# Sums of the first layer's softmax: TensorE products replaced by VectorE transposes and reductions for up to five of eight groups

## The chip, the core and the metric

One core of a Trainium2 chip runs the whole program. The engines have queues of their own: TensorE (PE, with weight loads as PEld), VectorE (DVE), ScalarE (ACT), GpSimd (POOL) and SyncE (SP), which issues most DMA transfers. They work side by side and wait for one another on semaphores. The metric is the device time of one execution in microseconds, the median of several runs. A profile is one execution recorded by the hardware profiler; its span is the time from the first to the last recorded instruction.

## The reference, cut to what matters

Two attention layers with a group normalisation ahead of each, on 8 batches of 32 x 32 positions (1024 tokens) with 512 channels, all in float32. The first layer has 16 heads of width 32, the second 4 heads of width 128 with position logits added to its scores.

```python
def _L0_conv_ref(x, w_qkv, w_proj, b_proj):      # first layer
    qkv = xt @ w_qkv                             # [B, 1024, 3 * 512], 16 heads of 32
    attn = jnp.einsum('bhid,bhjd->bhij', q * SCALE, k)
    attn = jax.nn.softmax(attn, axis=-1)
    out = jnp.einsum('bhij,bhjd->bhid', attn, v)
    out = out @ w_proj + b_proj
...
x = x + _L0_conv_ref(_gn(x), ...)
x = x + _L1_conv_ref(_gn(x), ...)                # second layer, with position logits
```

The softmax is computed without subtracting a maximum: the exponentials are summed over the keys, the unnormalised output is divided by that sum, and a bound on the sums is checked at the end of the program. The change is about the sums of the first layer.

## The kernel before, in words

**The order of the whole.** The program goes through the batches. Attention of the first layer for batch b is woven with other work: the second layer of batch b-1, and the first layer's projections for batch b+1. The weave is written out in the program: `side_by_side` takes steps of `attention_0` and, after each, as many pieces from the chain of other work as the costs that the pieces yield say. A piece of the other work is mostly one product of a projection: `seven` (L497) makes a projection from seven smaller products, into the PSUM tiles x (two), y (three) and z (two) (the names a, b, p with _q, _k, _v in the profile are the temporary tiles of that scheme). The products of one projection are issued by L421, sixteen records of the profile for one product; sums of products are made by VectorE (L511 a, L519 b), copies by ScalarE (L506, L525 p) and the last addition by GpSimd (L680). TensorE executes its instructions in the order in which the program lists them.

**Attention of the first layer** (`attention_0`, L796). A group is (m, h): four heads (m, in the order 0, 2, 1, 3) and one half of the queries (h, 512 of them); there are 8 groups per batch, numbered 0 to 7 here, and 64 in the program. Each group goes over 8 key blocks j of 128 keys. One step does:

- L809: scores of 128 keys by 512 queries for four heads, in `ps`, the one wide tile of PSUM (four banks)
- L824: their exponential, by ScalarE, from `ps` to a slot of `e_room`
- one step later, L835: four products with v, added up in `acc`
- L847: VectorE adds the exponentials to the group's first ones. After eight blocks that slot, `esum`, holds for each of four heads (`r`) the sums over the blocks, and 128 partitions are still to be added up.

**`e_room`** has three slots of 128 x 4 x 512. A group's first block takes a slot that stays its `esum`; the other two slots take turns. At the next group's first block its slot becomes the new sum slot and the old sum slot joins the turn; in it the next group's third block (j = 2) is written. So that exponential waits until the old `esum` has been read.

**The end of a group** (`finish`, L853, and `normalise`, L749). When the next group begins, TensorE multiplies `esum` by a matrix of ones, four products of 32 columns for the four heads (L857), which gives the sums over partitions, repeated in 32 partitions for each head, in a PSUM tile of the tag "acc". ScalarE copies them (L755), VectorE transposes them in blocks of 32 x 32 (L757), takes the reciprocal of one column in 32 (L772), records its bound (L775), and spreads it again by a transposing copy (`spread`, L787). GpSimd multiplies the output, which lies in `q`, with it (L761).

**The second layer** sums in another way. `added_up` (L763) transposes the 128 x 512 sum in blocks of 32 x 32 (L766) and reduces each run of 32 to one number (L767), which leaves 128 x 16 in `few`. `fold_up` (L1003) adds up the partitions that belong together by one product with the constant `fold` (L1008) for many groups at once, and inverts the result (L772). Then `quotient` (L1016) spreads each group's reciprocal (L787) and multiplies, on GpSimd or VectorE (L1024). For most batches the fold is in `closing` and the eight quotients in `quotients` (L1151); both run beside the first layer's projections for the coming batch, two quotients at a time, issued after the projection's VectorE instruction that `half_done` or `closed` names.

**The tag "rec"** is a ring of two tiles of 128 x 512. All of these take their tiles from it in turn: `su` and `tu` of `normalise`, the transposed tiles of `added_up`, the spare tiles of the folds, and the spread quotients of both layers. A tile that is asked for waits until the last reader of the tile before it in the same place is done; for a spread quotient that reader is the multiplication on GpSimd.

**Weights** come by DMA, issued by SP, into a ring of 16 tiles of the tag "w" (class `Stream`, L215).

## Time and profile before

| | |
|---|---|
| median of 3 runs | 3642.09 us (3640.19 to 3643.6) |
| profiled execution, its own time | 3640.86 us |
| span of the profile | 3639.1 us, clock 1.00 throughout |
| records of PE | 33882 |
| L857 sums | 512 records in 64 groups, 71.0 us busy |
| L755 copy of the sums (ACT) | 64, mean 585 ns |
| L757 transpose (DVE) | 64, mean 704 ns |
| L772 reciprocal, 128 x 16 (DVE) | 64, mean 257 ns |
| L787 spread (DVE), both layers | 128, mean 686 and 706 ns |
| L761 multiplication (POOL) | 64, mean 1672 ns |
| L1024 multiplication (POOL) | 48, mean 2052 ns |
| L766 and L767, transpose and reduction of the second layer (DVE) | 64 each, mean 712 and 685 ns |
| SP | issues DMA only |

How to read it: a group of instructions is one line of the kernel on one engine with one shape, as `out<-in` with partitions x elements, then the number of its records; then its busy time in us and the mean of one in ns; then the time that the engine stood idle just before such instructions, and who ended most of that. The ends of matmuls are modelled, so neighbours overlap on paper: a product of sixteen records lasts 1.90 but the next begins 1.72 or 1.83 us after it. For costs on TensorE the distance from start to start counts. Where the timeline joins neighbouring records, it gives the first one's start, the time to the end of the last and their number.

### The profile page before, as it was taken

What the parts mean: (1) busy time and instruction counts of PE and PEld (TensorE: products, weight loads), DVE (VectorE), ACT (ScalarE), POOL (GpSimd) and SP (SyncE); (2) the same over time, 40 slices, a digit from 0 to 9 for tenths busy, and PEclk for the clock granted to TensorE, in tenths of its full rate; (3) what the DMA queues carried; (4) which work ended last, traced back from release to release, by engine and by line L of the source; (5) the groups of instructions that cost most, each with busy time, mean ns of one, the idle gap of its engine ahead of it and who ended that gap; (6) DMA issues with size and microseconds to landing.
All of it is one profiled execution on the core that took longest, in us unless ns stands there. A gap on an engine that the chain in (4) does not pass through costs nothing.

```text
span 3639.1 us, 80878 instructions
## 1 busy us (share of the span) xinstructions
PE 3617.0 (99%) x33882; PEld 1232.4 (34%) x33882; DVE 2511.6 (69%) x2710; ACT 2000.6 (55%) x2285; POOL 1385.6 (38%) x880
## 2 busy tenths in 40 slices
PE   9999999999999999999999999999999999999998
PEld 4222243222433234332343323433234332323343
DVE  6788656796567955679556795667856668567546
ACT  3555666446664466544665446654566545656254
POOL 1343155231552316523174231742318312166255
PEclk9999999999999999999999999999999999999999
DMA  6233164242643426344363443625336133325376
GB/s 192 72 111 105 42 173 137 68 141 66 185 127 89 131 62 194 112 114 113 74 195 94 136 97 96 186 75 142 84 100 198 59 100 79 96 98 157 96 203 149
DMA packets 577316, 431.96 MB, mean 119 GB/s; under 512 B 274320, under 2 KB 467632, under 8 KB 575920
## 3 DMA queue, kind: packets, MB, share of 16 engines
q1 hardware_dynamic: 567952, 411.05, 41.1%
q0 software_dynamic: 2608, 13.70, 1.0%
q8 instruction: 269, 4.41, 0.5%
q10 hardware_dynamic: 6384, 1.97, 0.2%
q14 instruction: 103, 0.84, 0.1%
HBM read 334.30 MB, written 92.27 MB: 117 GB/s over the span
## 4 chain that ended last, share of the span: by engine, by line
PE 96%; DVE 2%; issue 1%; ACT 1%; POOL 0%; DMA 0%; SPq 0%; ACTq 0%; DVEq 0%; POOLq 0%
PE ps L809 15%; PE acc L835 14%; PE ps L1053 12%; PE acc L1067 12%; PE y_v L421 5%; PE y_q L421 4%; PE y_k L421 4%; PE x_v L421 3%; PE z_v L421 3%; PE z_q L421 3%; PE x_k L421 3%; PE x_q L421 3%; PE z_k L421 3%; PE y_wp L421 2%; PE y_wo L421 2%; PE sums L857 2%
## 5 line engine op out<-in xcount | busy, mean ns | idle before, releaser
L824 ACT ACTIVATE e_room<-ps 128x2048 f32<-128x2048 f32 x512 | 962.0, 1879 | 746.4 <-PE ps L809 724.9
L847 DVE TENSOR_TENSOR e_room<-e_room 128x2048 f32<-128x2048 f32 x448 | 1100.3, 2456 | 369.4 <-ACT e_room L824 367.6
L978 POOL TENSOR_TENSOR pos<-pos,columns 128x512 f32<-128x512 f32 x448 | 637.5, 1442 | 184.7 <-DMA pos<-pr 182.8
L809 PE MATMUL ps<-q,k 32*64 32x512 f32 x8192 | 592.5, 613 | 1.6 <-ACT e_room L824 1.6
L835 PE MATMUL acc<-e_room,v 128*32 128x512 f32 x4096 | 546.8, 604 | 0.0
L1053 PE MATMUL ps<-q,k 128*128 128x512 f32 x1024 | 526.4, 597 | 0.5 <-ACT ps L987 0.5
L1067 PE MATMUL acc<-e,v 128*128 128x512 f32 x1024 | 523.0, 593 | 0.0
L1056 ACT ACTIVATE e<-ps 128x512 f32<-128x512 f32 x512 | 305.7, 597 | 315.9 <-PE ps L1053 307.0
L1083 DVE TENSOR_TENSOR es<-es,e 128x512 f32<-128x512 f32 x384 | 278.7, 726 | 289.1 <-ACT e L1056 286.5
L761 POOL TENSOR_TENSOR q<-q,su 128x512 f32<-128x512 f32 x64 | 107.0, 1672 | 505.2 <-DVE su L787 478.2
L1067 PEld LDWEIGHTS acc<-e,v 128*128 128x128 f32 x1024 | 193.3, 190 | 247.6 <-issue 133.5
L1053 PEld LDWEIGHTS ps<-q,k 128*128 128x128 f32 x1024 | 190.8, 190 | 254.3 <-issue 229.7
L987 ACT COPY ps<-pos 128x512 f32<-128x512 f32 x448 | 264.9, 592 | 0.4
L809 PEld LDWEIGHTS ps<-q,k 32*64 32x64 f32 x8192 | 122.9, 129 | 396.9 <-issue 212.7
L835 PEld LDWEIGHTS acc<-e_room,v 128*32 128x32 f32 x4096 | 81.4, 108 | 412.1 <-issue 364.1
L680 POOL TENSOR_TENSOR k<-b_k,p_k 128x512 f32<-128x512 f32 x32 | 49.7, 1553 | 417.6 <-ACT p_k L525 406.8
L680 POOL TENSOR_TENSOR v<-b_v,p_v 128x512 f32<-128x512 f32 x32 | 51.5, 1609 | 342.9 <-ACT p_v L525 315.4
L1024 POOL TENSOR_TENSOR q<-q,su 128x512 f32<-128x512 f32 x48 | 97.5, 2052 | 191.8 <-DVE su L787 191.8
L680 POOL TENSOR_TENSOR q<-b_q,p_q 128x512 f32<-128x512 f32 x32 | 56.6, 1769 | 174.5 <-ACT p_q L525 160.0
L907 ACT COPY pos<-pp 32x512 f32<-32x512 f32 x128 | 104.6, 817 | 29.2 <-PE pp L898 28.0
L1081 DVE TENSOR_TENSOR es<-e,e 128x512 f32<-128x512 f32 x64 | 59.8, 934 | 67.1 <-ACT e L1056 67.1
L757 DVE STREAM_TRANSPOSE tu<-su 128x512 f32<-128x512 f32 x64 | 45.1, 704 | 77.5 <-ACT su L755 77.5
(241 smaller groups left out, 4551.1 us busy)
## 6 DMA issues: line engine op xcount, KB each, us to landing
pos<-pr SPq DMA_DIRECT2D x448, 256.0 KB, 3.5
w_qkv<-ws_qkv SPq DMA_DIRECT2D x168, 128.0 KB, 2.7
x1T<-d SPq DMA_DIRECT2D x32, 512.0 KB, 5.2
d<-x1T SPq DMA_DIRECT2D x32, 512.0 KB, 3.6
pc<-pos SPq DMA_DIRECT2D x32, 512.0 KB, 6.5
pr<-pos SPq DMA_DIRECT2D x32, 512.0 KB, 7.7
columns<-pc SPq DMA_DIRECT2D x64, 256.0 KB, 4.3
x2T<-d SPq DMA_DIRECT2D x32, 512.0 KB, 6.0
```

Of the source, the lines that this page charges most:

```text
L421: ins = nc.tensor.matmul(out[columns, :], weights[:, columns], moving, start=start, stop=stop, skip_group_check=open_sum,)
L680: nc.gpsimd.tensor_tensor(self.dst[1][1], s(b), s(p7), op=ALU.add)
L809: nc.tensor.matmul(ps[some, r, :], k[m][rows, j * P + 64 * i : j * P + 64 * i + 64], q[m][rows, h * NB : (h + 1) * NB], start=True, stop=True,
L824: exps[0] = nc.scalar.activation(e, ps, AF.Exp, scale=D0 ** -0.5)
L835: nc.tensor.matmul(acc[r * D0 : (r + 1) * D0, :], v[:, j, c0 : c0 + D0], e[:, r, :], start=(j == blocks[0]), stop=(j == blocks[-1]),)
L847: summed[0] = nc.vector.tensor_add(state["esum"], state["esum"], e)
L978: nc.gpsimd.tensor_tensor(self.rows[i], self.rows[i], self.columns[i // NT], op=ALU.add)
L987: self.copied = nc.scalar.copy(ps, rows)
L1053: scored[0] = nc.tensor.matmul(ps, k[h][:, keys], q[:, h, queries], start=False, stop=True, skip_group_check=True)
L1056: exps[0] = nc.scalar.activation(e, ps, AF.Exp, scale=1.0 / math.sqrt(D1))
L1067: nc.tensor.matmul(acc, v[:, j, h * D1 : (h + 1) * D1], e, start=(j == 0), stop=(j == NT - 1),)
L1083: added[0] = nc.vector.tensor_add(state["esum"], state["esum"], e)
```

## The change: what it does, and the diff

For the groups in `APART` the sums are not made by `finish`. In batch 0 there are none; in batch 1 they are the parts (2, 3) and (5, 6); in batches 2 to 6 (2, 3, 4) and (5, 6); in batch 7 (3, 4). That is 4 + 25 + 2 = 31 of 64 groups. A new class `Apart` holds a part:

- `take`: while the next group's first steps run, VectorE transposes each of the four rows of `esum` (128 x 512) into a tile of the ring "rec" and reduces it to 128 x 16 in the new buffer `few_0`. Rows 1 and 2 go in the first step, rows 3 and 4 in the second, issued after the VectorE instruction that `reader[0]` names.
- `fold_up`: once per part, four products with a 32-column matrix of `fold`, one for each row r, on 48 columns (a part of three groups) or 32 (of two); then one reciprocal with its bound for the whole part.
- `quotient`: for each group of the part a spread on VectorE and a multiplication on GpSimd.

The part (2, 3, 4) of batches up to 6 is put aside (`aside`): it is folded in the second layer's `closing`, directly after that layer's own fold, and its quotients are issued among the second layer's, one after each pair. The other parts are folded and multiplied in the steps after their last group. To make room for `few_0` the weights' ring has 15 tiles in place of 16. The bound checks are counted anew.

```diff
@@ -22,6 +22,8 @@
 SUM_BOUND = 1e20
 
 BLOCKS = 8
+
+APART = [(2, 3, 4), (5, 6)]
 
 
 @with_exitstack
@@ -132,7 +134,14 @@
     for t in mvs:
         nc.gpsimd.memset(t, 0.0)
 
+
+    def apart_of(b):
+        if b == 1:
+            return [(2, 3)] + APART[1:]
+        return [] if b == 0 else [(3, 4)] if b == B - 1 else APART
+
     n_checks = B * CC * NH + 2 * 4 + B - 2
+    n_checks -= sum(len(some) - 1 for b in range(B) for some in apart_of(b))
     checks = consts.tile([P, n_checks], F32, tag="checks", name="checks")
     check_at = [0]
 
@@ -243,11 +252,11 @@
                     m.kept = None
             elif rows:
                 for c in range(HC):
-                    t = mem.tile([P, HN], F32, tag="w", name=f"w_{m.name}_{n}_{i}_{c}", bufs=16)
+                    t = mem.tile([P, HN], F32, tag="w", name=f"w_{m.name}_{n}_{i}_{c}", bufs=15)
                     nc.sync.dma_start(t, src[:, c, :])
                     got.append(t)
             else:
-                t = mem.tile([P, HC, P], F32, tag="w", name=f"w_{m.name}_{n}_{i}", bufs=16)
+                t = mem.tile([P, HC, P], F32, tag="w", name=f"w_{m.name}_{n}_{i}", bufs=15)
                 nc.sync.dma_start(t, src[:, :, u * P : (u + 1) * P])
                 got = [t[:, c, :] for c in range(HC)]
             self.tiles[n, i] = got
@@ -793,10 +802,78 @@
     e_room = mem.tile([P, 3, HB, NB], F32, tag="e0", name="e_room", bufs=1)
     turn, sum_at = [0, 1], [2]
 
+    few_0 = mem.tile([P, HB, 3, NB // 32], F32, tag="few0", name="few_0", bufs=1)
+
+    class Apart:
+
+
+        def __init__(self, b, some):
+            self.b, self.some = b, some
+            self.groups = []
+            self.width = len(some) * (NB // 32)
+
+        def place(self, r):
+            return few_0[:, r, : len(self.some), :]
+
+        def take(self, m, h, esum, dst):
+            at = len(self.groups)
+            self.groups.append((m, h, dst))
+            for r0 in range(0, HB, 2):
+                turned = []
+                for r in (r0, r0 + 1):
+                    t = mem.tile([P, NB], F32, tag="rec", name=f"tu_0_{self.b}_{m}_{h}_{r}", bufs=2)
+                    with tc.issue_after(reader[0].ins) if r0 else nullcontext():
+                        nc.vector.transpose(t, esum[:, r, :])
+                    turned.append(t)
+                for r, t in zip((r0, r0 + 1), turned):
+                    nc.vector.tensor_reduce(
+                        few_0[:, r, at, :],
+                        t.rearrange("p (t c) -> p t c", c=32),
+                        axis=AX.X,
+                        op=ALU.add,
+                    )
+                yield
+
+        def fold_up(self):
+            name = f"0_{self.b}_{self.some[0]}"
+            su = bank(f"sums_{name}")[:, : self.width]
+            for r in range(HB):
+                ins = nc.tensor.matmul(
+                    su[r * D0 : (r + 1) * D0, :],
+                    fold[:, r, :],
+                    self.place(r).rearrange("p g t -> p (g t)"),
+                    start=True,
+                    stop=True,
+                )
+                tc.keep_in_program_order(ins)
+            spare = mem.tile([P, NB], F32, tag="rec", name=f"sp_{name}", bufs=2)
+            invert(self.place(0).rearrange("p g t -> p (g t)"), su, spare[:, : self.width])
+
+        def quotient(self, i, behind=None):
+            m, h, dst = self.groups[i]
+            su = mem.tile([P, NB], F32, tag="rec", name=f"su_0_{self.b}_{m}_{h}", bufs=2)
+            with tc.issue_after(behind.ins) if behind is not None else nullcontext():
+                spread(su, few_0[:, 0, i, :])
+            nc.gpsimd.tensor_tensor(dst, dst, su, op=ALU.mult)
+
     def attention_0(q, k, v, b, blocks=range(NT)):
 
         steps = [(m, h, j) for m in (0, 2, 1, 3) for h in range(NH) for j in blocks]
         state = {}
+        aparts = {i: part for some in apart_of(b) for part in [Apart(b, some)] for i in some}
+
+        def sums_apart(i, m, h, esum):
+            part = aparts[i]
+            together = i == 4 and b < B - 1
+            if together:
+                aside.append(part)
+            yield from part.take(m, h, esum, q[m][:, h * NB : (h + 1) * NB])
+            if together or i != part.some[-1]:
+                return
+            part.fold_up()
+            for i in range(len(part.some)):
+                yield
+                part.quotient(i)
 
         def front(m, h, j):
             name = f"0_{b}_{m}_{h}_{j}"
@@ -864,14 +941,23 @@
             normalise(q[m][:, h * NB : (h + 1) * NB], su, name)
 
         pending = None
+        ended, ending = 0, []
         for at in steps:
             if "ended" in state:
-                finish(*state.pop("ended"))
+                if ended in aparts:
+                    ending.append(sums_apart(ended, *state.pop("ended")))
+                else:
+                    finish(*state.pop("ended"))
+                ended += 1
+            for part in ending:
+                next(part, None)
             e = front(*at)
             if pending is not None:
                 back(*pending)
             pending = (*at, e)
             yield 2
+        for part in ending:
+            run(part)
         back(*pending)
         yield 1
         finish(*state.pop("ended"))
@@ -1141,9 +1227,13 @@
         for _ in range(3):
             next(last, None)
 
+        aside_0 = aside.pop() if aside else None
+
         def closing():
             if together:
                 fold_up(H1 * NH - 1, f"1_{b}")
+                if aside_0 is not None:
+                    aside_0.fold_up()
             else:
                 run(last)
             yield 0
@@ -1153,6 +1243,8 @@
                 late = half_done if i // 2 % 2 == 0 else closed
                 run(quotient(i, late[0], nc.gpsimd))
                 if i % 2:
+                    if aside_0 is not None and i // 2 < len(aside_0.some):
+                        aside_0.quotient(i // 2, begun[0])
                     yield 0
 
         ends.append(closing())
@@ -1584,7 +1676,7 @@
     plan += in_parts(WO, LAST_ALONE)
 
     states = [{} for _ in range(B)]
-    ends, left = [], []
+    ends, left, aside = [], [], []
     load_first(states[0])
     WV0.add_up([nc.gpsimd] * 2 + [nc.vector] * 2, nc.gpsimd, keep=True)
     fill_fold()
@@ -1690,6 +1782,7 @@
         else:
             run(chain(*rest))
     after_last(B - 1, states[B - 1])
+    assert check_at[0] == n_checks, (check_at[0], n_checks)
 
 
     close_wide()
```

## The prediction, made before the result was known

> **What bounds the kernel now.** I read the page's first part, then the chain of waits, then the stage windows, then the groups of instructions by line and shape, then the timeline of one group change.

> ```profile
> PE 3617.0 (99%) x33882; PEld 1232.4 (34%) x33882; DVE 2511.6 (69%) x2710; ACT 2000.6 (55%) x2285; POOL 1385.6 (38%) x880
> ...
> PE 96%; DVE 2%; issue 1%; ACT 1%; POOL 0%; DMA 0%; SPq 0%; ACTq 0%; DVEq 0%; POOLq 0%
> ```

> TensorE is busy 3617.0 of 3639.1 us and makes up 96% of the chain that ended last. So a TensorE instruction removed is worth its pitch, and TensorE made to wait costs the wait in full. One stage window in the middle (start:end, then busy us of PE, PEld, DVE, ACT, POOL, then clock and DMA) says the same of the steady state: no gap at all.

> ```profile
> 1456.00:1638.00 182.00, 182.00 (x1654) 64.47 (x1656) 126.62 (x147) 93.61 (x115) 64.04 (x44) 1.00 0.41 113
> ```

> The groups show who makes the sums now and what one instruction lasts:

> ```profile
> L847 DVE TENSOR_TENSOR e_room<-e_room 128x2048 f32<-128x2048 f32 x448 | 1100.3, 2456 | 369.4 <-ACT e_room L824 367.6
> ...
> L761 POOL TENSOR_TENSOR q<-q,su 128x512 f32<-128x512 f32 x64 | 107.0, 1672 | 505.2 <-DVE su L787 478.2 <-DVE avg L348 13.0 <-ACT e_room L824 11.5
> ...
> L1024 POOL TENSOR_TENSOR q<-q,su 128x512 f32<-128x512 f32 x48 | 97.5, 2052 | 191.8 <-DVE su L787 191.8
> ...
> L857 PE MATMUL sums<-e_room,ones 128*32 128x512 f32 x512 | 71.0, 596 | 1.2 <-ACT q L850 0.8 <-DVE e_room L847 0.4
> ...
> L757 DVE STREAM_TRANSPOSE tu<-su 128x512 f32<-128x512 f32 x64 | 45.1, 704 | 77.5 <-ACT su L755 77.5
> L767 DVE TENSOR_REDUCE few<-tu 128x16 f32<-128x512 f32 x64 | 43.8, 685 | 2.0
> ```

> L857 is 512 records for 64 groups, 8 per group (4 products of two passes each). TensorE hardly waits for them (1.2 us in all).

> Now group 5 of batch 3, just after its end: TensorE's queue, then GpSimd's.

> ```profile
> 1538.71 1.90 PE L421 MATMUL x_q<-x0T,w_qkv 128*32 128x512 f32 x16
> 1540.43 1.05 PE L857 MATMUL sums<-e_room,ones 128*32 128x512 f32 x8
> 1541.41 1.11 PE L809 MATMUL ps<-q,k 32*64 32x512 f32 x16
> ...
> 1545.05 1.90 PE L421 MATMUL z_q<-x0T,w_qkv 128*32 128x512 f32 x16
> 1546.88 1.11 PE L809 MATMUL ps<-q,k 32*64 32x512 f32 x16
> 1547.93 1.06 PE L835 MATMUL acc<-e_room,v 128*32 128x512 f32 x8
> ...
> 1550.64 1.11 PE L809 MATMUL ps<-q,k 32*64 32x512 f32 x16
> ```

> ```profile
> 1544.30 1.28 POOL L761 TENSOR_TENSOR q<-q,su 128x512 f32<-128x512 f32 x1 [5.34 <-DVE su L787]
> 1548.47 1.28 POOL L680 TENSOR_TENSOR q<-b_q,p_q 128x512 f32<-128x512 f32 x1 [2.89 <-DVE b_q L519]
> 1549.72 4.56 POOL L1024 TENSOR_TENSOR q<-q,su 128x512 f32<-128x512 f32 x2
> ```

> See two things. The score products of two following key blocks start at 1546.88 and 1550.64, back to back with other products. And GpSimd, at its leisure, multiplies layer 1's quotients exactly there.

> [...]the L847 addition lasts 2.29 us alone and 3.18 at 1544.54, beside a GpSimd multiplication; that takes 1.28 us alone and 3.28 where an addition holds it up (the 4.56 above for two).

> **Removed.** 31 groups (4 in batch 1, 5 in each of batches 2 to 6, 2 in batch 7) lose their four L857 products. At 1540.43 product to sums is 1.72 us (start to start), sums to scores 0.98; at 1545.05 product to scores is 1.83. One group's sums are worth 1.72 + 0.98 − 1.83 = 0.87 us of TensorE; 31 × 0.866 = −26.8 us, all on the path. The 31 ScalarE copies (L755, 0.585 each) are beside it: 0.

> **Added on TensorE.** 13 folds of four 48- or 32-column products. Nearest rows: layer 1's fold, pitch 0.42, and the 128-column position products (L891), 0.21 for four column tiles. From 0.2 to 0.45 each, no gain is possible; I take 0.3: +3.9 us (2.6 to 5.9).

> **Added on VectorE.** Per group four transposes at 0.71 and four reductions at 0.685: 5.6 us, 31 × 5.6 = 173. Out go 31 transposes, reciprocals and bound checks (0.70 + 0.26 + 0.32): −40; in come 13 reciprocals with checks of some 0.7: +9. So +142 us, busy 69% to 73%. Its cover is TensorE's own time, and mostly enough: in the 24 us after a group's end VectorE was busy 0.64 to 0.89 for groups 2 to 7 of the middle batches. If that cover is gone it shows through the waits below.

> **The added wait.** e_room has three slots. The exponential of the next group's third key block writes over the old sum, so it now waits for the fourth transposed row. The transposed rows lie in the tag "rec", a ring of two tiles shared with every spread quotient, and a quotient's tile comes free only when GpSimd has multiplied with it. In the built order, in batches 2 to 6 at the end of group 5, the ring holds before rows 3 and 4: layer 1's quotients A and B (m=2), then group 4's quotient C, whose spread itself waits for A. Row 3 waits for B, row 4 for C. GpSimd runs q (L680), A, B, C in this order, and q needs ScalarE's p_q copy after the z_q product. Queued behind row 4 on VectorE: two reductions and the next addition; on ScalarE that exponential with all after it; TensorE's scores of the fourth block need the one wide PSUM tile that it reads.

> From z_q's start (1545.05 = 0): p_q is copied by 2.55 (1547.02 + 0.58); L680 2.6 to 3.9; A to 5.2; B to 6.4; C's spread ends 5.9; C 6.4 to 7.7; row 4 7.7 to 8.4; exponential (1.88) 8.5 to 10.4; scores from 10.5. Without the wait they start at 1550.64 − 1545.05 = 5.59. TensorE stalls 4.9 us, in five batches: +24.5 us. In batch 1 only two layer-1 multiplications lie ahead of row 4: the exponential ends at 9.1, 3.5 us late; its groups 6 and 3 lose by the same count 1.4 and 0.3: +5.2. Groups 2, 3, 4 and 6 of the middle batches fit in; the set-aside fold may wait for a PSUM bank, 0.1 each: +0.5. In batch 7 sums waited before, up to 1 us: −0.5. Bounds of the stall: 3.5 to 6 us per batch, ±6 us in all; nothing if GpSimd should be early.

> **Moved.** The 31 multiplications on GpSimd come later, onto its free time (38% busy); those of part (2,3,4) run among layer 1's quotients, which is where C's wait comes from. Weights' ring of 15 in place of 16 tiles: some loads on SP start one tile later, 2.7 us each against 444 us per batch: 0, at worst a few tenths. All other TensorE work stays in its order.

> **Sum**, against the profiled execution's 3640.86 (span 3639.1): −26.8 + 3.9 + 24.5 + 5.2 + 0.5 − 0.5 = +6.8, so 3647.7. The median of runs is 3642.1, 1.2 higher: 3649.

> **Rivals.** R1, no stall: GpSimd gets through its queue in time, or VectorE's delay is hidden. For it: GpSimd has 62% idle, and the bulk of VectorE's added work does fit. Against it: L680 cannot start before z_q is done. 3642.1 − 26.8 + 3.9 = 3619. R1b, half the stall: −26.8 + 3.9 + 14.9 is −8.0, 3634.
> R2, ending slower: [...]An addition[...] holds GpSimd up by 3.28 − 1.28 = 2.0 us, five times +10; a_q, queued behind row 1 on VectorE, could add to it by making TensorE's y_q product wait, with some 1.4 us in hand. 3649 + 10 = 3659. It decides as soon as an addition starts within the 3.8 us in which A, B and C run. For it: that is what befell L1024 at 1549.72. Against: here the next addition is queued behind row 4.
> That the change is not carried out is excluded: the built order has 124 products fewer and 52 folds' more.

> **How the numbers follow.** Main case 0.58 (own range 3641 to 3657), R1 0.12, R1b 0.14, R2 0.16. Runs of this kernel can't tell less than about 0.2% (7.3 us) from no change, so same is 3634.8 to 3649.4. The main case lies at its upper edge: same 0.30, slower 0.26, faster 0.02; R1 faster 0.12; R1b faster 0.08, same 0.06; R2 slower 0.15, same 0.01. Faster 0.22, same 0.37, slower 0.41. The range leaves out R1 and the end of R2: 3630 to 3661.

> **What would show it.** L857 down to 264 records. In batches 2 to 6, at group 5's end, a gap of some 5 us on PE before L809's successor, released by the exponential, that by a transpose, that by GpSimd's quotient. VectorE near 2650 us busy, PE near 3594. Wrong if PE has no such gap (R1), if it is at another place, or if a fold shows over 0.5 us.

## The result and the profile after

The changed kernel takes 3654.66 us (median of 6 runs, 3651.59 to 3656.35), the kernel before 3640.84 on the same occasion (6 runs): ratio 1.0036, 95% interval 1.0024 to 1.0049. It is slower, by some 14 us. The profiled execution took 3654.94 with a span of 3653.1, 14.0 more than the span before.

First the page's busy line, the chain's shares and the group of the scores (busy us, mean ns | idle before, releaser):

```profile
PE 3605.1 (99%) x33738; PEld 1230.8 (34%) x33738; DVE 2601.5 (71%) x2873; ACT 1983.5 (54%) x2254; POOL 1389.8 (38%) x880
...
PE 95%; DVE 2%; ACT 1%; POOL 1%; issue 1%; DMA 0%; SPq 0%; ACTq 0%; DVEq 0%; POOLq 0%
...
L886 PE MATMUL ps<-q,k 32*64 32x512 f32 x8192 | 597.0, 617 | 29.6 <-ACT e_room L901 29.6
```

The scores' line has the news: its 8192 products now wait 29.6 us for the exponential, in place of 1.6 in the kernel before:

```profile
L809 PE MATMUL ps<-q,k 32*64 32x512 f32 x8192 | 592.5, 613 | 1.6 <-ACT e_room L824 1.6
```

Yet PE's busy time fell by only 11.9, where the removed products alone are worth 26.8. So TensorE not only stands, it also works more slowly somewhere. The groups of the new instructions:

```profile
L826 DVE STREAM_TRANSPOSE tu<-e_room 128x512 f32<-128x512 f32 x124 | 82.1, 690 | 8.7 <-POOL q L1110 5.2 <-POOL q L857 2.6
L829 DVE TENSOR_REDUCE few<-tu 128x16 f32<-128x512 f32 x124 | 77.0, 658 | 0.0
...
L934 PE MATMUL sums<-e_room,ones 128*32 128x512 f32 x264 | 38.6, 597 | 0.4 <-DVE e_room L924 0.4
```

The transposes of 31 x 4 rows are late by 8.7 us in all, and the releasers are GpSimd's multiplications. That is little time in a list of this size; what counts is where it lies. Group 5's end in batch 3, TensorE, GpSimd, VectorE and ScalarE in turn (start us, duration us):

```profile
1546.85 1.90 PE L430 MATMUL z_q<-x0T,w_qkv 128*32 128x512 f32 x16
...
1550.61 1.90 PE L430 MATMUL y_q<-f_xn,w_qkv 128*32 128x512 f32 x16
1557.26 2.01 PE L886 MATMUL ps<-q,k 32*64 32x512 f32 x16 [4.75 <-ACT e_room L901]
1559.20 1.94 PE L912 MATMUL acc<-e_room,v 128*32 128x512 f32 x8
1560.90 2.68 PE L430 MATMUL z_q<-x0T,w_qkv 128*32 128x512 f32 x16
...
1565.23 1.11 PE L886 MATMUL ps<-q,k 32*64 32x512 f32 x16
```

```profile
1549.54 1.28 POOL L689 TENSOR_TENSOR q<-b_q,p_q 128x512 f32<-128x512 f32 x1 [6.67 <-ACT p_q L534]
1550.77 2.50 POOL L1110 TENSOR_TENSOR q<-q,su 128x512 f32<-128x512 f32 x2
1553.22 1.26 POOL L857 TENSOR_TENSOR q<-q,su 128x512 f32<-128x512 f32 x1
```

```profile
1553.30 0.71 DVE L826 STREAM_TRANSPOSE tu<-e_room 128x512 f32<-128x512 f32 x1 [0.51 <-POOL q L1110]
1554.52 0.71 DVE L826 STREAM_TRANSPOSE tu<-e_room 128x512 f32<-128x512 f32 x1 [0.51 <-POOL q L857]
```

```profile
1555.33 1.88 ACT L901 ACTIVATE e_room<-ps 128x2048 f32<-128x2048 f32 x1 [5.87 <-DVE tu L826]
```

Read it backwards: the scores at 1557.26 wait for the exponential, that waited 5.87 us for row 4, row 4 for the multiplication C (L857), C for A and B (the two of L1110), these for q (L689), q for the copy after z_q. Counted from z_q's start at 1546.85, row 4 begins at 7.67, the exponential at 8.48, the scores at 10.41; 7.7, 8.5 and 10.5 were forecast.

Then look at the durations after the gap: scores 2.01 us in place of 1.11, the acc products 1.94 in place of 1.07. The stage windows (start:end, then busy us of PE, PEld, DVE, ACT, POOL, clock, DMA) say why:

```profile
1456.00:1638.00 182.00, 177.25 (x1570) 63.56 (x1568) 127.25 (x148) 89.63 (x112) 69.26 (x46) 0.98 0.36 103
1557.30:1562.40 5.10, 5.10 (x32) 1.08 (x36) 3.88 (x3) 1.88 (x1) 0.00 (x0) 0.50 0.01 3
```

The stage that was 182.00 of 182.00 at clock 1.00 now has the gap of 4.75 and a clock of 0.98; right after the gap the granted clock is 0.50. In the trace's clock record there are five such stretches ahead of the program's tail, each of 6.83 us, each with its start in the last 2.6 us of one of the five gaps.

Laying the starts of the same products in both traces side by side gives the difference before and after each place:

| term | forecast, us | measured, us |
|---|---|---|
| 31 groups' sums | −26.8 | −26.8 (31 x 0.865) |
| 13 folds | +3.9 | +1.5 (five set aside 0.22 each, the others 0.06) |
| gaps in batches 2 to 6 | +24.5 | +24.1 (5 x 4.83) |
| gaps in batch 1 | +5.2 | +4.6 (3.36 + 1.21) |
| waits for a PSUM bank | +0.5 | 0 |
| batch 7 | −0.5 | −0.5 |
| half clock after the five gaps | not counted | +12.0 (3.03, 2.52, 2.25, 2.12, 2.05) |
| sum | +6.8 | +14.9; the last products start 15.0 later, and the span is 14.0 longer |

The one microsecond between the last products and the span's end lies in the program's tail; it is not assigned.

### The profile page after: what moved, and what is told of

The parts are those of the page before. It is cut to its first block, busy times and chain, and to the rows that moved or that the text cites. A ratio compares the mean times of both kernels' runs of the same rounds, so it can differ in the third digit from the quotient of the medians.

```text
span 3653.1 us, 80736 instructions
## 1 busy us (share of the span) xinstructions
PE 3605.1 (99%) x33738; PEld 1230.8 (34%) x33738; DVE 2601.5 (71%) x2873; ACT 1983.5 (54%) x2254; POOL 1389.8 (38%) x880
## 4 chain that ended last, share of the span: by engine, by line
PE 95%; DVE 2%; ACT 1%; POOL 1%; issue 1%; DMA 0%; SPq 0%; ACTq 0%; DVEq 0%; POOLq 0%
PE ps L886 15%; PE acc L912 13%; PE ps L1139 12%; PE acc L1153 12%; PE y_v L430 5%; PE y_k L430 4%; PE y_q L430 4%; PE x_v L430 3%; PE z_v L430 3%; PE z_q L430 3%; PE x_k L430 3%; PE x_q L430 3%; PE z_k L430 3%; PE y_wp L430 2%; PE y_wo L430 2%; PE x_wp L430 2%
## 5 line engine op out<-in xcount | busy, mean ns | idle before, releaser
L924 DVE TENSOR_TENSOR e_room<-e_room 128x2048 f32<-128x2048 f32 x448 | 1075.9, 2401 | 401.7 <-ACT e_room L901 399.8
L1064 POOL TENSOR_TENSOR pos<-pos,columns 128x512 f32<-128x512 f32 x448 | 645.8, 1459 | 175.4 <-DMA pos<-pr 174.3
L886 PE MATMUL ps<-q,k 32*64 32x512 f32 x8192 | 597.0, 617 | 29.6 <-ACT e_room L901 29.6
L689 POOL TENSOR_TENSOR k<-b_k,p_k 128x512 f32<-128x512 f32 x32 | 49.4, 1544 | 536.7 <-ACT p_k L534 507.7
L689 POOL TENSOR_TENSOR v<-b_v,p_v 128x512 f32<-128x512 f32 x32 | 51.5, 1610 | 324.7 <-ACT p_v L534 300.0
L689 POOL TENSOR_TENSOR q<-b_q,p_q 128x512 f32<-128x512 f32 x32 | 62.9, 1965 | 292.0 <-ACT p_q L534 292.0
L770 POOL TENSOR_TENSOR q<-q,su 128x512 f32<-128x512 f32 x33 | 55.0, 1666 | 256.9 <-DVE su L796 231.9
L1110 POOL TENSOR_TENSOR q<-q,su 128x512 f32<-128x512 f32 x48 | 64.4, 1364 | 216.4 <-DVE su L796 216.0
L430 PE MATMUL y_q<-f_xn,w_q 128*32 128x512 f32 x768 | 91.3, 592 | 0.9 <-DVE a_q L520 0.9
```

What stands on the lines that cost most here:

```text
L430: ins = nc.tensor.matmul(out[columns, :], weights[:, columns], moving, start=start, stop=stop, skip_group_check=open_sum,)
L689: nc.gpsimd.tensor_tensor(self.dst[1][1], s(b), s(p7), op=ALU.add)
L886: nc.tensor.matmul(ps[some, r, :], k[m][rows, j * P + 64 * i : j * P + 64 * i + 64], q[m][rows, h * NB : (h + 1) * NB], start=True, stop=True,
L924: summed[0] = nc.vector.tensor_add(state["esum"], state["esum"], e)
L1064: nc.gpsimd.tensor_tensor(self.rows[i], self.rows[i], self.columns[i // NT], op=ALU.add)
```

## The experiments

In each the forecasts stand as they were written before the run.

**1. All rows in one step** (`at_once`): rows 3 and 4 follow rows 1 and 2 at once, so that no quotient's tile lies between them in the ring.

```diff
             for r0 in range(0, HB, 2):
...
-                    with tc.issue_after(reader[0].ins) if r0 else nullcontext():
+                    with nullcontext():
                         nc.vector.transpose(t, esum[:, r, :])
...
-                yield
+            yield
```

> All four rows of a group are transposed and reduced in the group's first step, so that no spread quotient lies ahead of rows 3 and 4 in the ring. Theory (ring wait, then half clock): the exponential of the third block waits for nothing on GpSimd, the five gaps of 4.8 us vanish, the clock stays at 1.00, and the time is that of before less 27.3 us of sums plus 1.5 us of folds: about 3615 (3612 to 3622). Rival (VectorE is too late for the extra 5.6 us per group, wherever they are put): a burst of 4.8 us ahead of the next addition makes TensorE wait at the same groups for a_q, b_q or the exponential; the time stays above 3640. Rival on the clock (the half-clock stretches come from something else than the gap): they stay, and the time is near 3627.

Measured: 3615.77 us (5 runs) against 3640.79, ratio 0.9932, interval 0.9918 to 0.9945. The clock and TensorE's waits, longest in total first (us, times, longest), then VectorE's rows at the end of group 5 in batch 3:

```profile
core 0: 3613.0 us, clock 1.000
```

```profile
PE turned L1349 <- DMA x_rows<-in_x: 4.9, 1, 4.9
PE ps L886 <- ACT e_room L901: 1.9, 4, 1.0
```

```profile
1531.25 0.69 DVE L826 STREAM_TRANSPOSE tu<-e_room 128x512 f32<-128x512 f32 x1
1531.86 1.24 DVE L829 TENSOR_REDUCE few<-tu 128x16 f32<-128x512 f32 x2
1533.02 1.29 DVE L826 STREAM_TRANSPOSE tu<-e_room 128x512 f32<-128x512 f32 x2
1534.23 1.24 DVE L829 TENSOR_REDUCE few<-tu 128x16 f32<-128x512 f32 x2
1535.39 2.28 DVE L924 TENSOR_TENSOR e_room<-e_room 128x2048 f32<-128x2048 f32 x1
```

All gaps and all stretches of half clock ahead of the tail are gone, with the same VectorE work (busy 2609.5 us). Row 4 is turned by 1534.31, before z_q's product has begun (1535.07 in this trace). So VectorE's load was not the cost; the rows' place behind the quotients, in the ring and in VectorE's queue alike, was.

**2. The third quotient later** (`c_later`).

```diff
-                    if aside_0 is not None and i // 2 < len(aside_0.some):
-                        aside_0.quotient(i // 2, begun[0])
+                    if aside_0 is not None and i // 2 != 2:
+                        aside_0.quotient(min(i // 2, 2), begun[0])
```

> Only the place of the set-aside part's third quotient is changed: it goes after the second layer's last pair in place of the third. Theory: ahead of row 4 there are two GpSimd multiplications in place of three, so row 4 may start at +6.5 us after the z_q product's start, the exponential ends at 9.2 and the gap is 3.6 us in place of 4.8, five times. As in batch 1 (gap 3.3 us, no change of clock) the clock then stays at 1.00: 3640.8 - 27.3 + 1.5 + 4.6 (batch 1) + 5 x 3.6 = 3637.6. Rival (the clock drops after any gap there, or from another cause): five half-clock stretches stay, 2.4 us each, and the time is near 3650. Rival (the wait is not on the ring): gap and time stay as in the change, 3655.

Measured: 3647.35 (20 runs, 3643.09 to 3652.23), ratio 1.0018 (1.0011 to 1.0024). The gaps are 3.54 us, five times: one multiplication less ahead of row 4 makes the gap 1.2 shorter, as a wait behind those multiplications demands. But my limit for the clock, an estimate from batch 1's gap of 3.3 us alone, was wrong: each of the five gaps brought a stretch of half clock, of 3.41 or 6.83 us. Without them 3637.6 was due; the 9.7 more are 1.9 per gap.

**3. A ring of their own** (`own_ring1`): rows go into a one-tile ring, each reduced before the next is turned, and the weights' ring falls from 15 to 13 tiles to make room.

```diff
-                    t = mem.tile([P, NB], F32, tag="rec", name=f"tu_0_{self.b}_{m}_{h}_{r}", bufs=2)
+                    t = mem.tile([P, NB], F32, tag="tu0", name=f"tu_0_{self.b}_{m}_{h}_{r}", bufs=1)
...
-                t = mem.tile([P, HC, P], F32, tag="w", name=f"w_{m.name}_{n}_{i}", bufs=15)
+                t = mem.tile([P, HC, P], F32, tag="w", name=f"w_{m.name}_{n}_{i}", bufs=13)
```

> The transposed rows get a ring of their own (one tile, each row reduced before the next is transposed); two more weight tiles make room (13). Theory A (the wait is on the ring alone): the gaps vanish, about 3615. Theory B (the queue order on VectorE carries the same wait): the spread of group 4's quotient stands ahead of row 4 in VectorE's queue and waits for GpSimd's first multiplication, so row 4 ends at +7.4 us, the exponential at 9.4, a gap of 3.8 us stays in five batches, and with the clock at 1.00 the time is about 3636 to 3639, with five drops of the clock about 3650. A weights' ring too short would show as TensorE waits on weight loads.

Measured: 3691.32, ratio 1.0143 (1.0127 to 1.0158). Its total says nothing on the rows, since the short weights' ring made TensorE wait 20.2 us for the DMA of a weight in batch 0 and put more delays into later v projections. But the gaps can be read: 3.63 us, five times, where theory B had 3.8. VectorE's queue at one of them shows it:

```profile
1130.90 0.67 DVE L825 STREAM_TRANSPOSE tu<-e_room 128x512 f32<-128x512 f32 x1
1132.62 0.71 DVE L796 STREAM_TRANSPOSE su<-few 128x512 f32<-128x512 f32 x1 [1.05 <-POOL q L1107]
1133.26 0.64 DVE L826 TENSOR_REDUCE few<-tu 128x16 f32<-128x512 f32 x1
1133.94 0.71 DVE L825 STREAM_TRANSPOSE tu<-e_room 128x512 f32<-128x512 f32 x1
```

Row 4 (1133.94) waits for no tile any more, but it stands in the queue behind a spread that waits for GpSimd. A ring of its own takes away one of two ways to the same wait; of the changed kernel's 4.8 us some 1.1 came by the ring alone.

**4. Groups 5 and 6 back on TensorE** (`no_56`).

```diff
-APART = [(2, 3, 4), (5, 6)]
+APART = [(2, 3, 4)]
```

> Only the parts that are set aside stay apart, (2,3,4), in batch 1 (2,3) and in batch 7 (3,4): 19 groups; groups 5 and 6 get their sums from TensorE as before. Theory: the five gaps belong to group 5 being apart, so they vanish with the clock drops: 3640.8 - 19 x 0.865 - 0.5 + 5 x 0.22 + 0.1 = about 3625. Rival (VectorE's added load as a whole is what costs): 19 of 31 parts of the loss stay, the time is about 3640.8 + 19/31 x 14 = 3649.

Measured: 3623.96, ratio 0.9952 (0.9937 to 0.9967); none of the five gaps is left. The 19 groups bring their 0.865 each, so the loss is all in the other part.

**5. More groups apart** (`wider`): experiment 1 with group 1 as well.

```diff
-APART = [(2, 3, 4), (5, 6)]
+APART = [(1, 2, 3, 4), (5, 6)]
...
-    few_0 = mem.tile([P, HB, 3, NB // 32], F32, tag="few0", name="few_0", bufs=1)
+    few_0 = mem.tile([P, HB, 4, NB // 32], F32, tag="few0", name="few_0", bufs=1)
```

> All four rows in the first step, and group 1 of batches 2 to 6 apart as well (36 groups in place of 31). In the kernel before VectorE was busy for 0.95 of the 24 us after group 1's end, so 1.2 us are free there for 5.6 us of added work. Theory (VectorE's free time is the cover, and here it is gone): the exponential of group 2's third block comes late, TensorE waits 1 to 4 us in five batches, and the time is above the 3615.8 of the same kernel without group 1: 3616 to 3635. Rival (VectorE's other work there can be put off): 5 x 0.865 less, 3611.4.

Measured: 3626.77, ratio to the kernel before 0.9963 (0.995 to 0.9977), so 11 us more than experiment 1. The size was right, the place was not: TensorE waits for VectorE's projection sums, not for the exponential.

```profile
PE y_q L430 <- DVE a_q L520: 6.7, 7, 1.1
...
PE y_q L430 <- DVE f_xn L469: 3.2, 5, 0.6
PE y_k L430 <- DVE a_k L520: 2.8, 6, 0.5
```

Group 1's five parts gave 5 x 0.865 back on TensorE and cost 2.15 us per batch at y_q and 0.7 at a later y_k. So in this one case VectorE's free time in the 24 us after a group's end was a fair measure: where it was 1.2 us, the added 5.6 did not fit.

**6. and 7. A gap without the change** (`gap_long`, `gap_short`): the kernel before, with ScalarE's exponential repeated at one place in batches 2 to 6 (n = 3 or 2).

```diff
+            if (m, h, j) == (3, 0, 2) and 2 <= b <= 6:
+                for _ in range(n):
+                    nc.scalar.activation(e, ps, AF.Exp, scale=D0 ** -0.5)
             exps[0] = nc.scalar.activation(e, ps, AF.Exp, scale=D0 ** -0.5)
```

> The kernel before, with the exponential of group 6's third block done four times over (the same values) in batches 2 to 6: ScalarE is 3 x 1.88 us late there, TensorE waits some 4.9 us, and nothing else is changed. Theory (a gap of that length makes TensorE's clock drop to half for one or two stretches of 3.41 us): 3640.8 + 5 x 4.9 + 5 x (0.5 to 3.0) = 3668 to 3680, with five half-clock stretches that begin near the end of the gaps. Rival (the drop belongs to the change, not to the gap): clock 1.00, 3640.8 + 24.5 = 3665.

> The same with the exponential done three times over: TensorE waits some 3.0 us, five times. Theory: [...]it costs its own length: 3640.8 + 15 = 3656, no half-clock stretch. Rival (any gap of some us can drop the clock): up to five stretches, to 3663 or more.

Both missed: 3644.54 (ratio 1.0010, 1.0004 to 1.0017) and 3645.26 (1.0014, 1.0005 to 1.0023), with no gap at all. TensorE in batch 3 of `gap_long`:

```profile
1549.51 1.90 PE L421 MATMUL y_q<-f_xn,w_qkv 128*32 128x512 f32 x16
1551.22 1.90 PE L421 MATMUL z_q<-x0T,w_qkv 128*32 128x512 f32 x16
1552.94 1.90 PE L421 MATMUL x_k<-x0T,w_qkv 128*32 128x512 f32 x16
1554.66 1.88 PE L421 MATMUL y_k<-f_xn,w_qkv 128*32 128x512 f32 x10
1556.47 1.12 PE L809 MATMUL ps<-q,k 32*64 32x512 f32 x16
```

Projection products were moved ahead of the scores. The two programs list TensorE's products in the same order, so the order on the engine isn't only that of the program's text, as the description of the kernel before has it; it seems to be settled when the program is built, with ScalarE's longer work in view. In the changed kernel TensorE's order stayed what it was, and its gap stayed open.

**8. The scan** (`gap_scan`), the same with delays of 3.0 to 5.6 us at five groups of batches 1 to 6; one execution.

> One look: the kernel before with the third block's exponential delayed by 3.0, 3.8, 4.4, 4.9 and 5.6 us in groups 3 to 7 of batches 1 to 6, so 30 gaps of some 2.3, 3.0, 3.6, 4.2 and 4.9 us at different phases. Theory: gaps of 2.3 and 3.0 never drop the clock, those of 3.6 to 4.2 at some phases, those of 4.9 nearly always; each drop lasts 3.41 us or twice that. Rival: drops have no relation to the length of the gap.

Most of these gaps were filled in the same way. Five of 3.76 us and five of 1.6 were left, in a kernel without the change: all five of 3.76 brought half clock, none of 1.6.

**9. and 10. The gap with the order pinned** (`gap_long2`, `gap_short2`): as 6 and 7, and the products from that block's scores on, three blocks long, keep the order of the kernel before.

```diff
+            pinned[0] = (m, h) == (3, 0) and j in (2, 3, 4) and 2 <= b <= 6
...
-            if in_place[0]:
+            if in_place[0] or pinned[0]:
                 tc.keep_in_program_order(ins)
```

> As gap_long, with TensorE's products around the place pinned in the order of the kernel before, so that nothing can be put into the gap: five gaps of some 4.9 us in batches 2 to 6 and no other change. Theory (a gap of that length drops the clock): 3640.6 + 5 x 4.9 = 3665 plus five times 2 to 3 us of half clock: 3675 to 3680, with five half-clock stretches. Rival (the drop comes with the change and not with the gap): clock 1.00, 3665.

> The same with gaps of some 3.0 us. Theory: below the 3.3 us that left the clock alone in batch 1, so the clock stays at 1.00 and a gap costs its own length: 3640.6 + 15 = 3656. Rival[...]: up to five half-clock stretches, 3661 to 3668.

Measured: `gap_long2` 3676.02, ratio 1.0098 (1.0081 to 1.0115), with five gaps of 5.05 us: 35.9 us over its own runs of before, of which 25.3 are the gaps and 10.6, 2.1 each, is more. Five stretches of half clock come with them. TensorE in batch 3, and the window right after the gap (clock 0.67):

```profile
1556.09 1.90 PE L423 MATMUL y_q<-f_xn,w_qkv 128*32 128x512 f32 x16
1563.05 1.95 PE L812 MATMUL ps<-q,k 32*64 32x512 f32 x16 [5.05 <-ACT e_room L832]
1564.92 1.88 PE L843 MATMUL acc<-e_room,v 128*32 128x512 f32 x8
1566.63 1.89 PE L423 MATMUL z_q<-x0T,w_qkv 128*32 128x512 f32 x16
1568.35 1.89 PE L423 MATMUL x_k<-x0T,w_qkv 128*32 128x512 f32 x16
1570.17 1.11 PE L812 MATMUL ps<-q,k 32*64 32x512 f32 x16
```

```profile
1563.10:1568.20 5.10, 5.10 (x40) 1.09 (x44) 3.46 (x2) 1.88 (x1) 0.00 (x0) 0.67 0.00 0
```

So the slower products belong to the gap and to nothing else in the change. `gap_short2` took 3669.72, ratio 1.0081 (1.0064 to 1.0097), not 3656: with gaps of 3.15 us its profile has four stretches of half clock. The rival was right here, though the time lies 1.7 us above its range.

**11. The pinned scan** (`gap_scan2`): gaps of five lengths at five groups of batches 1 to 6, pinned; one execution.

> One look: pinned as well, gaps of some 1.7, 2.3, 3.0, 3.6 and 4.2 us at five groups of batches 1 to 6, 30 in all. Theory: no half-clock stretch after the gaps of up to 3.0 us, one or two of 3.41 us after those of 3.6 and 4.2 us. Rival: the stretches come at other places or after short gaps as often.

With the other runs' gaps this gives how often half clock followed (looked for within 2.6 us before and 1.6 us after a gap's end):

| gap, us | from | half clock after |
|---|---|---|
| 1.6 to 2.5 | the two scans | 0 of 17 |
| 3.03 to 3.30 | `gap_short2`, `gap_scan2`, batch 1 of three kernels | 10 of 14 |
| 3.5 to 3.9 | `c_later`, `own_ring1`, the two scans | 24 of 25 |
| 4.1 to 5.1 | the changed kernel, `gap_long2`, `gap_scan2` | 11 of 11 |

No gap of up to 2.48 us brought half clock and most from 3.03 us on did, so the limit of 3.3 us, my estimate from the one gap in batch 1, was too high. In between it matters where a gap lies. In each of the nine profiles with more than one stretch, the starts of all stretches are whole multiples of 3.413 us apart, to 0.001 us. If TensorE's time ahead of the tail is cut into windows by that grid, half clock began right after every window in which TensorE stood idle for 2.03 us or more (45 of 45) and, apart from one stretch, after none with 1.87 us or less; of the five windows with 1.88 to 1.99 us, one was followed by it. The gap of 3.29 us in batch 1 of the changed kernel is cut by the grid into 1.90 and 1.39 us and brought nothing; the same gap in `filled` (experiment 12) is cut into 0.69 and 2.61 and brought a stretch. A stretch lasted 6.83 us or more where TensorE stood idle for 0.56 us or more in the stretch's first window, and 3.41 us where for 0.54 or less, with the same one exception.

That exception is in the profile of `no_56`: a stretch of 6.83 us at 3189 us, 2.3 us after a gap of only 1.04, which all other profiles have without one. It was real: the products there came 3.0 us later for it, and this execution took 3626.70 us where the other three took 3623.43 to 3623.99. What set it off is open.

**12. The gap filled** (`filled`): the changed kernel, with products of weight zero added into y_q's sum at the gap.

```diff
         product(y, 2, False)
+        if name in filled:
+            for _ in range(10):
+                for g in range(P // 32):
+                    ins = nc.tensor.matmul(
+                        y[32 * g : 32 * g + 32, :],
+                        zeros,
+                        fs[2][:, 0, :],
+                        start=False,
+                        stop=True,
+                        skip_group_check=True,
+                    )
+                    tc.keep_in_program_order(ins)
```

> The changed kernel, with ten times four products of weight zero added to y_q's sum (it does not change) at the place of the gap in batches 2 to 6: 4.3 us of TensorE's work into gaps of 4.8. The wait and its length stay. Theory (the half clock comes from TensorE standing idle): the gaps shrink to some 0.5 us, the clock stays at 1.00, the half-clock stretches' 2 to 3 us per batch are won back, and the time is 3654.7 - 12.0 = 3642.7. Rival (the stretches have another cause): 3655. The same if products with zero weights do not count as work.

Measured: 3666.54, ratio 1.0068 (1.0055 to 1.0082). I had the filler's size wrong: four such products take 0.87 us in two passes, not 0.43, so it overfills each gap by 3.75 us. What it was for can be read all the same: TensorE in batch 3, the exponential there, and the window right after the added products (clock 1.00):

```profile
1555.01 8.77 PE L543 MATMUL y_q<-f_xn,zeros 128*32 128x512 f32 x80
1563.71 1.11 PE L901 MATMUL ps<-q,k 32*64 32x512 f32 x16
1564.75 1.06 PE L927 MATMUL acc<-e_room,v 128*32 128x512 f32 x8
```

```profile
1558.06 1.88 ACT L916 ACTIVATE e_room<-ps 128x2048 f32<-128x2048 f32 x1 [5.91 <-DVE tu L841]
```

```profile
1563.70:1568.80 5.10, 5.10 (x60) 1.43 (x56) 2.59 (x2) 1.88 (x1) 0.00 (x0) 1.00 0.01 2
```

Row 4 and the exponential are as late as before, but TensorE isn't idle, and the scores take 1.11 us at once. Against the changed kernel the products after the five gaps win back 3.03, 2.52, 2.25, 2.12 and 2.05 us, to the hundredth what the half clock had cost there. The one stretch ahead of the tail, 3.41 us, comes with the gap of 3.29 us in batch 1, into which nothing was put.

## Why the prediction came out as it did

**The bound** was right: TensorE. Each group's sums are worth 0.865 us on it, and in experiments 1 and 4 all of that reached the end.

**The added wait** was right, in its place (group 5's end, batches 2 to 6), its chain, its size (4.83 against 4.9) and in batch 1 (4.6 against 5.2). Experiments 1 and 2 show that it comes from the quotients ahead of the rows, but they don't part the ring from VectorE's queue. Experiment 3 does: the queue carries 3.6 us of it even without the ring, and some 1.1 us is the ring's alone.

**What the wait costs** is the step that failed. The prediction said that "TensorE made to wait costs the wait in full"; it costs more. After each of the five gaps TensorE's granted clock was 0.50 for 6.83 us, which cost 12.0 us in all. The prediction put nothing down for it. Forecast was a difference of +6.9 us between the medians, measured +13.8; the half clock is more than the whole of that distance (the folds, cheaper than forecast, give some back), and it turned a change at the edge of no difference into a slower one. That 3654.66 still lies within the main case's range of 3641 to 3657 is luck: its width was meant for the length of the stall, which came out as forecast. A gap of 4.8 us was not needed for the half clock: of the six gaps of 3.03 us in `gap_scan2` five brought it.

**The folds** were over-priced, 3.9 against 1.5: I had taken 0.3 each. The trace gives 0.22 for the set-aside folds, near the low end of the range of 0.2 to 0.45, and 0.06 for the four 32-column products of the other folds, well below it. Products this narrow stand in the trace before too: the second layer's own folds (L1008) have some of 16, 32 and 64 columns, at 247, 234 and 247 ns.

**VectorE** grew by 90 us of busy time, not 142. The transposes and reductions sum to 159; the L924 additions became shorter (1075.9 us against 1100.3), probably because fewer of them ran beside GpSimd: 216 of the 448 before (mean 2.64 us) and 192 after (2.55), where one without GpSimd beside it took 2.29 in both traces. It changes nothing on the path.

**R2**, an addition that holds GpSimd up at the same place, was not the cause: A, B and C took 1.25 to 1.26 us each in batch 3, where R2 put 3.28 on one of them, y_q's product did not wait for a_q, and the added gap was 4.8 us in all five batches. The measured time lies between the main case's 3649 and R2's 3659, for another reason than R2's; the durations of the products after the gap tell the two apart. R1 did not happen here, but it is what experiment 1 makes of the change.

**The version that is better than both** is experiment 1: 3615.77 us, 25 us less than before and 39 less than the changed kernel, for one `yield` moved and one issue order dropped.

## What to carry to other kernels

When work moves to an engine with free time, follow its buffers: a ring that is shared with tiles which a slow engine releases hands on that engine's delay (here 4.83 us at group 5's end), and so does a queue in which the new instruction stands behind such a tile's user (3.63 us in `own_ring1`). Take such tiles one straight after the other, ahead of the shared ones. Price a gap on a saturated TensorE at its length plus the slow products after it (here 4.75 to 4.77 us and another 2.05 to 3.03), and look at their durations and the granted clock first when the measured loss is larger than the gaps.
